# Recommender attention on one core: the user stage keeps the rows of 128 users whole, in three SBUF buffers, and reads their sums in place

## The chip, the cores and the metric

The kernel runs on one core of a Trainium2 chip. The metric is the device time of one execution in microseconds (us), lower is better. A program on one core has engines that run side by side: PE (TensorE, matmuls), DVE (VectorE), ACT (ScalarE), POOL (GpSimd) and SP (SyncE). Each works through its own queue in order, and they wait for each other by semaphores. A transfer by indices ("indirect DMA") is issued by POOL: one instruction fetches one row of a DRAM table for each of 128 partitions.

## What is computed

For 16,384 users there is a history of 100 items and one target item. Each item has a row h of 128 numbers: 64 of an embedding and 2 x 32 that come from an attention over 32 neighbouring items. The core of the reference, cut:

```python
a_sus = _neighbor_attn(E_in, near_full)      # softmax over 32 neighbours, for each item
a_inf = _neighbor_attn(E_out, near_full)
h = concat([E_hist[history], a_sus[history], a_inf[history]])      # 16384 x 100 x 128
t = concat([E_tgt[target], a_inf[target], a_sus[target]])          # 16384 x 128
x = h * t[:, None, :]
z = relu(einsum('bld,hd->blh', x, W1) + b1)
scores = einsum('blh,h->bl', z, W2[0])
exp_A = exp(scores) * ((history != target[:, None]) & (history != 0))
denom = sum(exp_A, -1) ** 0.5
s = sum(h * (exp_A / denom[:, None])[..., None])                   # one number over all users
pred = cosine(broadcast(s), t);  return sigmoid(pred)
```

Since s is a sum over all of a row's 128 numbers too, a history item enters it only by the sum of its row, weighted by its attention.

## The kernel before

**Table stage (lines 111 to 238).** For each item the attention over its neighbours is computed, and a row of W = 129 numbers is written to a DRAM table: the row's sum first, then its 128 numbers. The change does not touch this stage.

**User stage (lines 249 to 399).** Users are taken 128 at a time, one on each partition; there are UC = 128 such batches, called "users" c below. The 100 history items of a batch are taken in NG = 25 groups of LG = 4. A step s is one group: c, g = divmod(s, 25), 3,200 steps in all. The program's order on each engine is written out by hand in the loop at line 377 (a manual schedule: each engine gets its instructions in the order in which the loop names them). For a step:

- `gather(s)` (line 299): four indirect DMAs on POOL, one for each item, bring 128 rows of 129 numbers into an SBUF tile `h` of the pool `u_h`. The pool has HBUF = 20 such tiles, so POOL can be twenty groups ahead, and then waits until the group twenty steps back has been read.
- `turn(s)` (line 316): PE transposes the four blocks of 128 x 128 (without the sum's column) into one PSUM tile `hT_ps`; the pool `ps_t` has three, shared with two small uses.
- `times_target(s)` (line 322): DVE multiplies the tile by the target's transposed row (`xT`, line 325, called a "product" below), and copies the four sums into `hsum` (line 328). That copy is the last reader of the tile `h`.
- `hidden(s - 3)` (line 335, LAG = 3): PE multiplies by W1 (`z_ps`, line 337, issued as two matmuls) and ACT applies the relu (line 339).
- `scored(s - 6)` (line 341): PE multiplies by W2 into one row of the PSUM tile `bank` (line 345, two matmuls).

So a step has eight matmuls on PE with eight weight loads. Once for each user there are the target's row (`target_rows`, a gather on POOL; `target_work`), and, when its 25 groups are scored, `weights`, `exponents` and `ended`: the exponentials of the scores, the mask, their sum, and their product with `hsum` (line 369).

An instruction carries one semaphore wait. Where it has to wait for more, the further waits stand ahead of it in its queue as an instruction of their own, a "separate wait". In the program before, POOL has one ahead of nearly each group's first gather (the tile's readers on DVE, beside PE), PE one for each group's transposes, DVE one for over half of its products, ACT some.

Of the kernel before, what the change touches and what calls it, by code (L numbers as in the profile page):

```python
# [10 lines left out]
F32 = mybir.dt.float32  # L11
# [3 lines left out]
AF = mybir.ActivationFunctionType  # L15
# [3 lines left out]
P = 128  # L19
# [4 lines left out]
D = 128  # L24
# [19 lines left out]
LG = 4  # L44
NG = L // LG
W = 1 + D
LAG = 3
M = 2
HBUF = 20

# [3 lines left out]
def kernel(  # L54
# [56 lines left out]
    with (  # L111
# [137 lines left out]
    with (  # L249
        tc.manual_schedule(engines={E.PE, E.Activation, E.DVE, E.SP, E.Pool}),  # L250
        tc.tile_pool(name="u_in", bufs=4) as u_in,
        tc.tile_pool(name="u_t", bufs=3) as u_t,
        tc.tile_pool(name="u_h", bufs=HBUF) as u_h,
        tc.tile_pool(name="u_x", bufs=6) as u_x,
        tc.tile_pool(name="u_z", bufs=6) as u_z,
        tc.tile_pool(name="u_s", bufs=3) as u_s,
        tc.tile_pool(name="ps_t", bufs=3, space=bass.MemoryType.PSUM) as ps_t,
        tc.tile_pool(name="ps_z", bufs=3, space=bass.MemoryType.PSUM) as ps_z,
        tc.tile_pool(name="ps_s", bufs=2, space=bass.MemoryType.PSUM) as ps_s,
    ):  # L260
        users, hists = {}, {}
        rows, got, hT, xT, z = {}, {}, {}, {}, {}

        def history_of(i):
            hists[i] = u_in.tile([P, BSUB, L], I32, name="hidx")
            nc.sync.dma_start(hists[i], hist_v[i])

        def target_rows(c):
            t = u_t.tile([P, D], F32, name="t")
            nc.gpsimd.indirect_dma_start(  # L270
                out=t,
                out_offset=None,
                in_=ttab[0:ITEMS, :],
                in_offset=bass.IndirectOffsetOnAxis(ap=tidx[:, c : c + 1], axis=0),
            )
            users[c] = {"t": t, "hidx": hists[c // BSUB][:, c % BSUB, :]}

        def target_work(c):
            u = users[c]
            t = u["t"]  # L280
            tT_ps = ps_t.tile([P, LG, P], F32, name="hT_ps")
# [14 lines left out]
            u["keep"] = keep  # L296
            u["hsum"] = u_s.tile([P, L], F32, name="hsum")

        def gather(s):
            c, g = divmod(s, NG)  # L300
            rows[s] = u_h.tile([P, LG, W], F32, name="h")
            got[s] = []
            for q in range(LG):
                l = g * LG + q
                got[s].append(
                    nc.gpsimd.indirect_dma_start(  # L306
                        out=rows[s][:, q, :],
                        out_offset=None,
                        in_=table,
                        in_offset=bass.IndirectOffsetOnAxis(  # L310
                            ap=users[c]["hidx"][:, l : l + 1], axis=0
                        ),
                    )
                )

        def turn(s):
            c, g = divmod(s, NG)
            hT[s] = ps_t.tile([P, LG, P], F32, name="hT_ps")
            for q in range(LG):
                nc.tensor.transpose(hT[s][:, q, :], rows[s][:, q, 1:W], ident)  # L320

        def times_target(s):
            c, g = divmod(s, NG)
            xT[s] = u_x.tile([D, LG, P], F32, name="xT")
            nc.vector.tensor_tensor(  # L325
                xT[s], hT.pop(s), users[c]["tT"].to_broadcast([D, LG, P]), ALU.mult
            )
            copy = nc.vector.tensor_copy(  # L328
                users[c]["hsum"][:, g * LG : (g + 1) * LG],
                rows.pop(s)[:, :, 0:1].rearrange("p q o -> p (q o)"),  # L330
            )
            for one in got.pop(s):
                tc.declare_no_dep(copy.ins, one.ins, reason="TensorE has read the row")

        def hidden(s):
            z_ps = ps_z.tile([HID, LG, P], F32, name="z_ps")
            nc.tensor.matmul(z_ps, w1T, xT.pop(s), start=True, stop=True)  # L337
            z[s] = u_z.tile([HID, LG, P], F32, name="z")
            nc.scalar.activation(z[s], z_ps, AF.Relu, bias=b1_sb)  # L339

        def scored(s):
            c, g = divmod(s, NG)
            if g == 0:
                users[c]["bank"] = ps_s.tile([NG, LG, P], F32, name="bank")
            nc.tensor.matmul(  # L345
                users[c]["bank"], pick[:, g, :], z.pop(s), start=g == 0, stop=g == NG - 1
            )

        def weights(c):
            flat = u_t.tile([NG, LG, P], F32, name="flat")  # L350
            nc.scalar.copy(flat, users[c].pop("bank"))  # L351
            users[c]["flat"] = flat

        def exponents(c):
            flat = users[c].pop("flat")
            score = ps_t.tile([P, LG, P], F32, name="hT_ps")
# [20 lines left out]
        for s in range(last + 2 * LAG + 6):  # L377
# [15 lines left out]
            done, left = divmod(s - 2 * LAG - NG, NG)  # L393
# [93 lines left out]
```

## Time and profile before

| what | value |
|---|---|
| time, median of 3 runs | 36161.68 us (36157.8 to 36170.7) |
| the profiled execution's own time | 36158.99 us |
| its span in the profile | 36157.2 us |
| busy in the span | POOL 25713.0 us (71%), PE 9955.5 (28%), DVE 6910.6 (19%), ACT 2692.6 (7%) |
| mean granted TensorE clock | 0.854 |

How to read the rows that follow. In the page's slices, each digit is an engine's busy share in a fortieth of the span, in tenths. A row of a group is: line, engine, operation, output<-inputs with shapes, xcount | busy us in all, mean ns of one | idle time of the engine just before these instructions, and what ended most of it. A row of the timeline is: start, duration, engine, line, operation, count, and in brackets the idle time before it with what ended it. "issue" means that the engine waited for nothing that the profile shows, "remote" that the releaser is not known. PE's rows are in two parts, PEld for weight loads and PE for matmuls. Ends of matmuls are modelled.

### The profile page before, as it was taken

The page shows a single profiled execution, that of the slowest core. Times are in us where ns is not written, and L with a number is a line of the kernel's source. Part 1 is how long each engine was busy: PE and PEld are TensorE (multiplying, and loading weights), DVE is VectorE, ACT ScalarE, POOL GpSimd, SP SyncE. Part 2 cuts the span into 40 slices and gives each one's busy share as a digit, 9 for nine tenths or more (in the row PEclk, how much of TensorE's full clock was granted, in tenths as well). Part 3 has the DMA queues.
Part 4 walks back from the last instruction along what each step waited for, and adds up shares of the span by engine and source line. Part 5 has one row for each costly group of instructions (what it writes and reads, how often), then busy time and mean ns, then how long its engine had stood idle before and what let it go on. Part 6 is the DMA issues. An engine that isn't in the chain of part 4 may idle for free.

```text
span 36157.2 us, 104181 instructions
## 1 busy us (share of the span) xinstructions
PE 9955.5 (28%) x26243; PEld 3219.9 (9%) x26243; DVE 6910.6 (19%) x9965; ACT 2692.6 (7%) x5700; POOL 25713.0 (71%) x25446
## 2 busy tenths in 40 slices
PE   0000000000000000000255555555555555555555
PEld 0000000000000000000011111111111111111111
DVE  2222222222222222222111111111111111111111
ACT  0000000000000000000011111111111111111111
POOL 7777777777777777777666666666666666666666
PEclk9999999999999999999877777777777777777777
DMA  1111111111111111111111111111111111111111
GB/s 42 29 27 27 27 28 29 27 27 27 28 29 28 27 27 28 27 29 25 40 47 47 47 47 47 47 46 47 47 47 47 46 47 46 47 47 47 46 46 43
DMA packets 1027956, 1362.32 MB, mean 38 GB/s; under 512 B 559904, under 2 KB 614432, under 8 KB 1027360
## 3 DMA queue, kind: packets, MB, share of 16 engines
q0 software_dynamic: 814080, 1265.42, 14.4%
q10 hardware_dynamic: 151056, 51.51, 0.8%
q1 hardware_dynamic: 62224, 38.72, 0.4%
q8 instruction: 218, 3.57, 0.0%
q14 instruction: 378, 3.10, 0.0%
HBM read 1315.31 MB, written 51.50 MB: 38 GB/s over the span
## 4 chain that ended last, share of the span: by engine, by line
POOL 37%; another core or an unknown queue 29%; PE 18%; issue 13%; DVE 2%; ACT 1%; DMA 0%; POOLq 0%; SPq 0%; ACTq 0%; DVEq 0%
POOL v L144 37%; PE z_ps L337 7%; PE bank L345 6%; PE hT_ps L320 5%; DVE xT L325 1%; ACT z L339 1%; DVE hsum L328 0%; DMA v<-in_egeo_dram,nidx 0%; PE hT_ps L358 0%; POOL h L306 0%; PE hT_ps L282 0%; ACT flat L351 0%; DVE tT L284 0%; DVE keep L293 0%
## 5 line engine op out<-in xcount | busy, mean ns | idle before, releaser
L306 POOL DMA_INDIRECT h<-table,hidx x12800 | 12107.2, 946 | 6300.4 <-issue 3830.4
L144 POOL DMA_INDIRECT v<-in_egeo_dram,nidx x12512 | 13484.1, 1078 | 4013.5 <-issue 3964.1
L325 DVE TENSOR_TENSOR xT<-hT_ps,tT 128x512 f32<-128x512 f32 x3200 | 2198.7, 690 | 15477.9 <-remote 9681.0
L282 PE MATMUL hT_ps<-ident,t 128*128 128x128 f32 x128 | 46.3, 362 | 17780.0 <-DMA t<-ttab,tidx 17522.1
L337 PE MATMUL z_ps<-xT,w1T 128*128 128x512 f32 x6400 | 4177.9, 741 | 1833.5 <-ACT z L339 1463.2
L320 PE MATMUL hT_ps<-ident,h 128*128 128x128 f32 x12800 | 2520.1, 328 | 5521.0 <-DVE xT L325 3984.9
L345 PE MATMUL bank<-z,pick 128*25 128x512 f32 x6400 | 3978.8, 709 | 0.0
L339 ACT ACTIVATE z<-z_ps,b_sb 128x512 f32<-128x512 f32 x3200 | 2149.8, 687 | 15996.4 <-remote 7924.9
L159 DVE TENSOR_TENSOR prod<-v,own_ps 128x4096 f32<-128x4096 f32 x196 | 864.4, 4410 | 12916.3 <-DMA v<-in_egeo_dram,nidx 12850.6
L320 PEld LDWEIGHTS hT_ps<-ident,h 128*128 128x128 f32 x12800 | 1621.4, 163 | 8660.4 <-DVE xT L325 4994.7
L282 PEld LDWEIGHTS hT_ps<-ident,t 128*128 128x128 f32 x128 | 19.1, 149 | 17919.3 <-issue 17586.5
L176 ACT ACTIVATE ex<-sc,top 128x32 f32<-128x32 f32 x782 | 227.8, 291 | 16993.6 <-DVE top L170 12332.7
L192 DVE TENSOR_TENSOR wv<-v,ex 128x1024 f32<-128x1024 f32 x782 | 1378.3, 1875 | 315.9 <-ACT ex L176 299.5
L337 PEld LDWEIGHTS z_ps<-xT,w1T 128*128 128x128 f32 x6400 | 1175.1, 230 | 2056.4 <-ACT z L339 1647.9
L166 DVE TENSOR_REDUCE sc<-prod 128x128 f32<-128x4096 f32 x196 | 864.4, 4410 | 6.7
L200 DVE TENSOR_REDUCE att<-wv 128x128 f32<-128x4096 f32 x196 | 864.1, 4409 | 6.0
L345 PEld LDWEIGHTS bank<-z,pick 128*25 128x25 f32 x6400 | 433.4, 109 | 3095.3 <-issue 3095.3
L328 DVE COPY hsum<-h 128x4 f32<-128x4 f32 x3200 | 568.9, 178 | 0.0
L358 PE MATMUL hT_ps<-ident,flat 25*128 25x25 f32 x512 | 65.8, 249 | 1051.5 <-ACT flat L351 714.5
L270 POOL DMA_INDIRECT t<-ttab,tidx x128 | 121.1, 946 | 65.9 <-issue 64.1
L358 PEld LDWEIGHTS hT_ps<-ident,flat 25*128 25x128 f32 x512 | 51.5, 170 | 1190.1 <-ACT flat L351 777.2
L176 ACT ACTIVATION_READ_ACCUMULATOR ex<-sc,top 128x1 f32 x782 | 146.0, 187 | 0.0
(55 smaller groups left out, 855.7 us busy)
## 6 DMA issues: line engine op xcount, KB each, us to landing
h<-table,hidx POOLq DMA_INDIRECT x12800
v<-in_egeo_dram,nidx POOLq DMA_INDIRECT x12512
table<-row ACTq DMA_DIRECT2D x22, 1096.5 KB
own<-in_egeo_dram SPq DMA_DIRECT2D x23, 544.0 KB
row<-in_ehist_dram SPq DMA_DIRECT2D x23, 544.0 KB
ttab<-in_etgt_dram ACTq DMA_DIRECT2D x1, 12500.0 KB
ttab<-row ACTq DMA_DIRECT2D x22, 544.0 KB
hidx<-in_history_dram SPq DMA_DIRECT2D x32, 200.0 KB
```

Of the source, the lines that this page charges most:

```text
L144: nc.gpsimd.indirect_dma_start(out=v[:, m, k].rearrange("p t d -> p (t d)"), out_offset=None, in_=egeo, in_offset=bass.IndirectOffsetOnAxi ...
L159: nc.vector.tensor_tensor(prod[:, 0:n].rearrange("p m k t d -> p m k (t d)"), v.rearrange("p m k t d -> p m k (t d)"), own_ps[:, 0:n].to_b ...
L166: nc.vector.tensor_reduce(sc[:, 0:n].rearrange("p m t k -> p m k t"), prod[:, 0:n], AX.X, ALU.add)
L192: nc.vector.tensor_tensor(wv[:, m, t].rearrange("p d k -> p k d"), subs[b]["v"][:, m, :, t, :], ex[:, m, t, :].rearrange("p (k o) -> p k o ...
L200: nc.vector.tensor_reduce(att[:, 0:n], wv[:, 0:n], AX.X, ALU.add)
L306: nc.gpsimd.indirect_dma_start(out=rows[s][:, q, :], out_offset=None, in_=table, in_offset=bass.IndirectOffsetOnAxis(ap=users[c]["hidx"][: ...
L320: nc.tensor.transpose(hT[s][:, q, :], rows[s][:, q, 1:W], ident)
L325: nc.vector.tensor_tensor(xT[s], hT.pop(s), users[c]["tT"].to_broadcast([D, LG, P]), ALU.mult)
L328: copy = nc.vector.tensor_copy(users[c]["hsum"][:, g * LG : (g + 1) * LG], rows.pop(s)[:, :, 0:1].rearrange("p q o -> p (q o)"),)
L337: nc.tensor.matmul(z_ps, w1T, xT.pop(s), start=True, stop=True)
L339: nc.scalar.activation(z[s], z_ps, AF.Relu, bias=b1_sb)
L345: nc.tensor.matmul(users[c]["bank"], pick[:, g, :], z.pop(s), start=g == 0, stop=g == NG - 1)
```

## The change

- `h` is now a tile of a whole user, 100 rows of 129 numbers on each partition, and there are HOLD = 3 of them. A gather writes its row into it.
- The copy into `hsum` is gone. `ended(c)` reads the sums in place, in the user's tile. That read is now the last reader, so that the waits of the gathers of user c + 3 for the rows of user c come down to one, ahead of its first gather.
- The tiles `hT`, `z_ps`, `xT` and `z` are no longer taken from pools but are fixed rings of TB = 2, ZP = 3, XB = 4 and ZB = 4. The target's transposition and the exponents use a PSUM tile of their own (`e_ps`).
- The order of a step on PE is now `scored(s - 5)`, `hidden(s - 2)`, `turn(s)` instead of `turn(s)`, `hidden(s - 3)`, `scored(s - 6)`. With the rings' sizes, what an instruction has to wait for is then already implied by an earlier wait in its own queue, or is the one wait that it carries; `declare_no_dep` tells the framework which dependences are implied (`in_order`: one engine writes both in its order).

The diff, cut to its core:

```diff
-LAG = 3
 M = 2
-HBUF = 20
+HOLD = 3
+TB = 2
+XB = 4
+ZP = 3
+ZB = 4
+LH = 2
+LS = LH + ZP
...
-        tc.tile_pool(name="u_h", bufs=HBUF) as u_h,
-        tc.tile_pool(name="u_x", bufs=6) as u_x,
-        tc.tile_pool(name="u_z", bufs=6) as u_z,
+        tc.tile_pool(name="u_h", bufs=HOLD) as u_h,
+        tc.tile_pool(name="u_r", bufs=1) as u_r,
...
+        hT = [ps_r.tile([P, LG, P], F32, name=f"hT{i}") for i in range(TB)]
+        z_ps = [ps_r.tile([HID, LG, P], F32, name=f"z_ps{i}") for i in range(ZP)]
+        xT = [u_r.tile([D, LG, P], F32, name=f"xT{i}") for i in range(XB)]
+        z = [u_r.tile([HID, LG, P], F32, name=f"z{i}") for i in range(ZB)]
+        def in_order(one, other):
+            tc.declare_no_dep(one.ins, other.ins, reason="one engine writes both in its order")
...
         def gather(s):
             c, g = divmod(s, NG)
-            rows[s] = u_h.tile([P, LG, W], F32, name="h")
...
+            if g == 0:
+                rows[c] = u_h.tile([P, L, W], F32, name="h")
+            for l in range(g * LG, (g + 1) * LG):
+                one = nc.gpsimd.indirect_dma_start(
+                    out=rows[c][:, l, :],
...
+                got[c, l] = one
+                if c >= HOLD:
+                    tc.declare_no_dep(
+                        one.ins,
+                        turned[c - HOLD, l].ins,
+                        reason="the sums of these users are read after their rows are turned",
+                    )
...
-            hT[s] = ps_t.tile([P, LG, P], F32, name="hT_ps")
-            for q in range(LG):
-                nc.tensor.transpose(hT[s][:, q, :], rows[s][:, q, 1:W], ident)
+                turned[c, l] = nc.tensor.transpose(hT[s % TB][:, q, :], rows[c][:, l, 1:W], ident)
+                if s >= TB:
+                    in_order(turned[c, l], turned[(s - TB) // NG, (s - TB) % NG * LG + q])
...
-            copy = nc.vector.tensor_copy(
-                users[c]["hsum"][:, g * LG : (g + 1) * LG],
-                rows.pop(s)[:, :, 0:1].rearrange("p q o -> p (q o)"),
-            )
...
-            nc.vector.tensor_tensor(ea, ea, u["hsum"], ALU.mult)
+            sums = nc.vector.tensor_tensor(
+                ea, ea, rows.pop(c)[:, :, 0:1].rearrange("p l o -> p (l o)"), ALU.mult
+            )
+            for l in range(L):
+                tc.declare_no_dep(
+                    sums.ins, got.pop((c, l)).ins, reason="TensorE has read the row"
+                )
...
                 gather(s)
+            if 0 <= s - LS < last:
+                scored(s - LS)
+            if 0 <= s - LH < last:
+                hidden(s - LH)
+            if s < last:
                 turn(s)
                 times_target(s)
-            if 0 <= s - LAG < last:
-                hidden(s - LAG)
-            if 0 <= s - 2 * LAG < last:
-                scored(s - 2 * LAG)
```

More of the change, by code (lines that the diff above doesn't have):

```diff
@@ L252 @@
         tc.tile_pool(name="u_t", bufs=3) as u_t,
-        tc.tile_pool(name="u_h", bufs=HBUF) as u_h,
-        tc.tile_pool(name="u_x", bufs=6) as u_x,
-        tc.tile_pool(name="u_z", bufs=6) as u_z,
+        tc.tile_pool(name="u_h", bufs=HOLD) as u_h,
+        tc.tile_pool(name="u_r", bufs=1) as u_r,
         tc.tile_pool(name="u_s", bufs=3) as u_s,
-        tc.tile_pool(name="ps_t", bufs=3, space=bass.MemoryType.PSUM) as ps_t,
-        tc.tile_pool(name="ps_z", bufs=3, space=bass.MemoryType.PSUM) as ps_z,
+        tc.tile_pool(name="ps_r", bufs=1, space=bass.MemoryType.PSUM) as ps_r,
+        tc.tile_pool(name="ps_e", bufs=1, space=bass.MemoryType.PSUM) as ps_e,
         tc.tile_pool(name="ps_s", bufs=2, space=bass.MemoryType.PSUM) as ps_s,
@@ L261 @@
         users, hists = {}, {}
-        rows, got, hT, xT, z = {}, {}, {}, {}, {}
+        rows, got, turned, times, first, second = {}, {}, {}, {}, {}, {}
+        hT = [ps_r.tile([P, LG, P], F32, name=f"hT{i}") for i in range(TB)]
[4 more added lines that the diff above has]
+            tc.declare_no_dep(one.ins, other.ins, reason="one engine writes both in its order")
         def history_of(i):
@@ L280, in target_work @@
             t = u["t"]
-            tT_ps = ps_t.tile([P, LG, P], F32, name="hT_ps")
+            tT_ps = ps_e.tile([P, LG, P], F32, name="e_ps")
             nc.tensor.transpose(tT_ps[:, 0, :], t, ident)
@@ L296, in target_work @@
             u["keep"] = keep
-            u["hsum"] = u_s.tile([P, L], F32, name="hsum")
         def gather(s):
             c, g = divmod(s, NG)
-            rows[s] = u_h.tile([P, LG, W], F32, name="h")
-            got[s] = []
+            if g == 0:
[3 more added lines that the diff above has]
+                    out=rows[c][:, l, :],
+                    out_offset=None,
+                    in_=table,
+                    in_offset=bass.IndirectOffsetOnAxis(
+                        ap=users[c]["hidx"][:, l : l + 1], axis=0
+                    ),
+                )
[6 more added lines that the diff above has]
+                    )
@@ L303, in gather, with turn @@
+        def turn(s):
+            c, g = divmod(s, NG)
             for q in range(LG):
                 l = g * LG + q
[L305 to L312, printed above, removed]
-                    )
-                )
@@ L335, in hidden @@
[L335 to L339, printed above, removed]
+            times[s] = nc.vector.tensor_tensor(
+                xT[s % XB], hT[s % TB], users[c]["tT"].to_broadcast([D, LG, P]), ALU.mult
+            )
+            for q in range(LG - 1):
+                tc.declare_no_dep(
+                    times[s].ins, turned[c, g * LG + q].ins, reason="TensorE turns them in order"
+                )
@@ L341, in scored, with hidden @@
+            if s >= XB:
+                in_order(times[s], times.pop(s - XB))
+        def hidden(s):
+            first[s] = nc.tensor.matmul(
+                z_ps[s % ZP], w1T, xT[s % XB], start=True, stop=True
+            )
+            if s >= ZP:
+                in_order(first[s], first.pop(s - ZP))
+            second[s] = nc.scalar.activation(z[s % ZB], z_ps[s % ZP], AF.Relu, bias=b1_sb)
+            if s >= ZB:
+                in_order(second[s], second.pop(s - ZB))
         def scored(s):
@@ L345, in scored @@
             nc.tensor.matmul(
-                users[c]["bank"], pick[:, g, :], z.pop(s), start=g == 0, stop=g == NG - 1
+                users[c]["bank"], pick[:, g, :], z[s % ZB], start=g == 0, stop=g == NG - 1
             )
@@ L355, in exponents @@
             flat = users[c].pop("flat")
-            score = ps_t.tile([P, LG, P], F32, name="hT_ps")
+            score = ps_e.tile([P, LG, P], F32, name="e_ps")
             for q in range(LG):
@@ L376 @@
         target_work(0)
-        for s in range(last + 2 * LAG + 6):
+        for s in range(last + LS + 6):
             c, g = divmod(s, NG)
@@ L384 @@
                 gather(s)
+            if 0 <= s - LS < last:
[3 more added lines that the diff above has]
+            if s < last:
                 turn(s)
                 times_target(s)
-            if 0 <= s - LAG < last:
-                hidden(s - LAG)
-            if 0 <= s - 2 * LAG < last:
-                scored(s - 2 * LAG)
             if s < last and g == 15 and c + 1 < UC:
                 target_work(c + 1)
-            done, left = divmod(s - 2 * LAG - NG, NG)
+            done, left = divmod(s - LS - NG, NG)
             if 0 <= done < UC and left == 0:
```

10 lines of the change are left out of this document (3 added, 7 removed).

## The prediction

> **What bounds the kernel now.** I read the page first: the shares by slice and the groups.
>
> ```profile
> span 36157.2 us, 104181 instructions
> PE   0000000000000000000255555555555555555555
> POOL 7777777777777777777666666666666666666666
> L306 POOL DMA_INDIRECT h<-table,hidx x12800 | 12107.2, 946 | 6300.4 <-issue 3830.4
> L270 POOL DMA_INDIRECT t<-ttab,tidx x128 | 121.1, 946 | 65.9 <-issue 64.1
> ```
>
> The first half of the span is the stage that builds the table. It is not touched. The user stage, where PE works, issues 12,800 + 128 row gathers on POOL. How fast could POOL issue them? That is in the timeline of POOL alone, here the first and the last history gather of the stage and one run of gathers with the stall behind it.
>
> ```profile
> 17530.95 0.95 POOL L306 DMA_INDIRECT h<-table,hidx  x1 [3.94 <-DMA hidx<-in_history_dram]
> ...
> 25014.49 0.94 POOL L306 DMA_INDIRECT h<-table,hidx  x1 [2.36 <-PE hT_ps L320]
> 25015.74 0.95 POOL L306 DMA_INDIRECT h<-table,hidx  x1 [0.31 <-issue]
> ...
> 25048.27 0.94 POOL L306 DMA_INDIRECT h<-table,hidx  x1 [0.30 <-issue]
> 25054.00 0.94 POOL L306 DMA_INDIRECT h<-table,hidx  x1 [4.79 <-PE hT_ps L320]
> ...
> 36092.54 0.95 POOL L306 DMA_INDIRECT h<-table,hidx  x1 [0.30 <-issue]
> ```
>
> From 25014.49 to 25048.27 there are 27 steps: 1.2511 us a gather. The stage's 12,927 steps would take 16,173 us at that pace; they took 36092.54 - 17530.95 = 18,561.6. So POOL stalls for 2,389 us, 18.7 us for each of 128 users, whose 101 gathers need 126.4 us. These stalls are waits for a buffer of rows: POOL is twenty groups (of four rows) ahead and waits for PE and DVE. A change that gives POOL more buffers helps only if PE and DVE can keep POOL's pace of 5.06 us a group (126.4 / 25). So the next view is what PE and DVE do while POOL runs. The timeline of all engines near the stage's start, where POOL's twenty buffers are still free and POOL waits for nobody:
>
> ```profile
> 17564.00 0.69 DVE L325 TENSOR_TENSOR xT<-hT_ps,tT 128x512 f32<-128x512 f32 x1 [5.45 <-PE hT_ps L320]
> ...
> 17600.27 0.69 DVE L325 TENSOR_TENSOR xT<-hT_ps,tT 128x512 f32<-128x512 f32 x1 [20.85 <-remote]
> ...
> 17601.02 1.12 PE L320 MATMUL hT_ps<-ident,h 128*128 128x128 f32 x4 [12.56 <-issue]
> ...
> 17606.57 0.69 ACT L339 ACTIVATE z<-z_ps,b_sb 128x512 f32<-128x512 f32 x1 [21.71 <-remote]
> ...
> 17607.31 2.08 PE L337 MATMUL z_ps<-xT,w1T 128*128 128x512 f32 x2 [5.17 <-issue]
> ...
> 17609.31 1.90 PE L345 MATMUL bank<-z,pick 128*25 128x512 f32 x2
> ...
> 17622.67 0.69 DVE L325 TENSOR_TENSOR xT<-hT_ps,tT 128x512 f32<-128x512 f32 x1 [21.63 <-remote]
> ...
> 17628.98 0.69 ACT L339 ACTIVATE z<-z_ps,b_sb 128x512 f32<-128x512 f32 x1 [21.73 <-remote]
> ```
>
> Up to 17564.00 DVE has made six products in 33 us, at POOL's pace. Then it falls back. PE's work for a group is over at 17611.2, and DVE's operand has stood in PSUM for long, since PE may be three groups ahead (three PSUM tiles). Yet DVE starts its next product 22.40 us after the last one, and ACT its next 22.41 us after its last, both idle and with a releaser that the profile can't name ("remote"). What is late is the news from PE that its instructions have ended. 22.40 us for the 16 PE instructions of a group (eight weight loads, eight matmuls) is 1.40 us each. Two windows of the groups view (122 us near the start, then 34.8 us of the run shown above) say how much gets through while POOL runs:
>
> ```profile
> L325 DVE TENSOR_TENSOR xT<-hT_ps,tT 128x512 f32<-128x512 f32 x6 | 4.2, 692 | 121.2 <-remote 107.4 <-PE hT_ps L320 13.8
> L306 POOL DMA_INDIRECT h<-table,hidx x94 | 88.9, 946 | 31.5 <-issue 30.0 <-DMA h<-table,hidx 1.2 <-PE bank L345 0.3
> ...
> L325 DVE TENSOR_TENSOR xT<-hT_ps,tT 128x512 f32<-128x512 f32 x6 | 4.1, 692 | 17.4 <-PE z_ps L337 8.3 <-remote 7.6 <-PE hT_ps L320 1.4
> L306 POOL DMA_INDIRECT h<-table,hidx x28 | 26.5, 946 | 10.6 <-issue 7.3 <-PE hT_ps L320 2.4 <-remote 0.6
> ```
>
> Six products in 122 us (20.3 us each) where POOL has run without a break; six in 34.8 us right after a stall. And where POOL has ended for good, in the timeline behind the last gather and in the groups from 36100 to 36140:
>
> ```profile
> 36095.31 0.68 DVE L325 TENSOR_TENSOR xT<-hT_ps,tT 128x512 f32<-128x512 f32 x1
> ...
> 36098.80 1.90 PE L345 MATMUL bank<-z,pick 128*25 128x512 f32 x2
> ...
> 36133.35 0.69 DVE L325 TENSOR_TENSOR xT<-hT_ps,tT 128x512 f32<-128x512 f32 x1 [1.65 <-PE hT_ps L320]
> ...
> 36135.76 0.69 DVE L325 TENSOR_TENSOR xT<-hT_ps,tT 128x512 f32<-128x512 f32 x1 [1.65 <-PE hT_ps L320]
> ...
> 36136.52 1.04 PE L345 MATMUL bank<-z,pick 128*25 128x512 f32 x2
> ...
> L325 DVE TENSOR_TENSOR xT<-hT_ps,tT 128x512 f32<-128x512 f32 x15 | 10.4, 692 | 26.0 <-PE hT_ps L320 26.0
> ```
>
> Here a group takes 2.41 us (36133.35 to 36135.76), fifteen of them lie between 36100 and 36140, with the same instructions and the same waits. So the stage swings between two paces: while POOL gathers, PE's ends reach DVE and ACT at 20 to 22 us a group, after a credit of some groups that a stall has bought; while POOL stands still, a group takes 2.41 us. POOL's short stalls are what lets the rest catch up. They are not waste that more buffers remove.
>
> **The change, part by part.** The time is made against the profiled execution, 36158.99 us (span 36157.2 and 1.8 around it), 2.7 below the median of 36161.68; 0.2% of that is 72 us, about what a measurement can tell.
>
> *Instructions.* The hsum copies go, and in the built programs the separate waits go from 3,198 to none on PE (transposes), 1,796 to none on DVE, 380 to none on ACT (relu) and 3,149 to 94 on POOL.
>
> ```profile
> L325 DVE TENSOR_TENSOR xT<-hT_ps,tT 128x512 f32<-128x512 f32 x3200 | 2198.7, 690 | 15477.9 <-remote 9681.0
> L328 DVE COPY hsum<-h 128x4 f32<-128x4 f32 x3200 | 568.9, 178 | 0.0
> ```
>
> The copies' 569 us lie beside 15,478 us of idle time that DVE has ahead of its products: worth nothing. The same idle time covers the strided read of the sums, once a user; without that cover the 128 reads would still be a few tens of us. The waits that go cost PE and DVE no time where POOL is still (2.41 us a group with them). What they cost while POOL runs no row shows alone. The bounds: nothing, if the 1.40 us belong to PE's 16 instructions, which all stay; everything that POOL loses, 2,389 us, if they belong to the waits. I take nothing, since the sixteen account for the 22.40 and since the tail has the same waits at 2.41; the other end is a rival.
>
> *Buffers.* POOL no longer waits group by group. It writes three users' rows freely, then needs, ahead of each further user c + 3, the sums' read of user c, which DVE does behind the tenth product of user c + 1. So there is one stall a user instead of about four short ones (18.7 / 4.79), and a run is 126.4 us long. Behind POOL's one wait all its gathers are queued, those of the target rows too; nobody lacks rows meanwhile, since two users and more lie ready.
>
> *Products in a run of 126.4 us.* Six in the first 34.8, then (126.4 - 34.8) / 20.3 = 4.5: 10.5. PE's lead is shorter (two transposed groups instead of three, and the first matmul now stands ahead of the next transposes): I take one off, 9.5. Below: 5.6, if each costs 22.40 from the start. Above: 14, if the credit after a long stall is twice that of a short one.
>
> *The stall.* 25 - 9.5 = 15.5 groups at 2.41 are 37.4 us; 3 more for its start (1.8 us from the last gather's end at 36093.49 to the first product at 36095.31, and PE's bank matmuls at first 1.90 us a pair instead of 1.04): 40.5 us a user, against 18.7 before.
>
> *The sum.* Three users filled freely: 3 x 126.4 = 379 us, in which some 23 products get done (six by 17564, then one in 20.3); the read that POOL waits for stands behind the 35th: 12 x 2.41 + 3 = 32. Then 125 users at 126.4 = 15,800, with 124 stalls of 40.5 = 5,022 between them. When POOL ends, 55.5 groups are left (3,200 less the 3,135 ahead of user 124's read, less 9.5): 134 us, and 21 from the last product at 36135.76 to the end of the span. 17,531 + 379 + 32 + 15,800 + 5,022 + 134 + 21 = 38,919; with 1.8 around it **38,921 us**, given as 38,920, 7.6% slower.
>
> *A rule beside this.* The Trainium skill, "Perfetto Trace Analysis", section "Optimization Strategy", says that the same gap repeating on the engine that should be saturated can mean too little memory for the next tile, buffer count among it. By that rule three whole users of rows would end POOL's stalls, and the sum would be the first rival's below. The trace does not agree: with all twenty buffers free the products came 22.40 us apart.
>
> **The rivals.**
>
> *The waits are the cause (faster).* If the separate waits make PE's news late, the pace under a running POOL falls below 5.06 us a group, POOL never stalls, and the stage is bound by its gathers: 36,159 - 2,389 = 33,770, less some 20 us of shorter tail: 33,750. That decides from 5.06 us downward. For it: up to 17564.00 the products kept POOL's pace, and just there DVE's products begin to wait separately, since their first six buffers are used up. Against it: the tail's 2.41. The Trainium skill, "TensorE: Matmul & The Clock Gate", section "The cost: per-tile semaphore tail", has 26.3 ns for each increment that a matmul makes on completion; by that figure the six increments of a group are an estimated 0.16 us, nothing would be late, and this rival's time would follow. The trace disagrees where POOL runs (22.40 us a group).
>
> *No memory in the pace.* If a long stall buys as much for each us as the short ones do now, 18.7 us a user still do: 36,160, no change. Against it: the pace falls from 5.8 us (34.8 / 6) to 20.3 us as a run goes on.
>
> *The stall at the slow clock.* If PE stays at the pace of 17601 (1.12 + 2.08 + 1.90 = 5.10 us a group) through the stall, it is 15.5 x 5.10 + 3 = 82 us, and the time 44,070. Against it: at the tail the bank pair is back at 1.04.
>
> **How the numbers follow.** Forecast 0.81, waits 0.13, no memory 0.03, slow clock 0.03. The forecast's own bounds: 14 products in a run give a stall of 11 x 2.41 = 26.5 and 37,190; 5.6 in a run give 19.4 x 2.41 + 3 = 50, and four of those groups at 5.10 another 11: 61, and 41,460. The range is 37,100 to 41,450; it leaves out the waits' case and the slow clock's. Faster 0.14 (the waits, and a third of "no memory"), same 0.02, slower 0.84.
>
> **What would show it.** In the timeline of POOL: runs of 101 gathers 1.25 us apart, and one idle time of about 40 us ahead of each user's first gather. In the timeline of DVE: products about 20 us apart late in such a run, 2.4 us apart in the idle time. The products' idle time should still be put down to "remote". It is wrong if the products follow at 5 us or less while POOL runs (the waits were the cause), or if the stall is near 19 us.

## The result, and the profile after

The changed kernel takes 39,756.5 us (median of 5, 39,739 to 39,761) against 36,162.8 (median of 5) before: a ratio of 1.0993, 95% interval 1.0981 to 1.1004. It is slower, as forecast; the profiled execution (39,756.5 us) is 835 us above the sum of 38,921. One thing is needed to read the later numbers: the runs came in two conditions that no kernel set, told apart by the table stage, which all kernels share. In the first (the result, E1 to E4, E11) a gather of that stage takes 1.40 us on average and before takes 36,160 to 36,250 us; in the second (E5 to E10, E12) it takes 1.25 us throughout and before takes 31,867 to 31,896. Every run is set against the kernel before in its own condition.

The page of the changed kernel (span, slices, groups), and from the waits view of POOL in the window from 18,000 to 39,000 us its largest row (engine, line, what it waited for: us in all, times, longest):

```profile
span 39754.7 us, 92550 instructions
PE   0000000000000000004444444444444444444444
POOL 7777777777777777775555555555555555555554
L315 POOL DMA_INDIRECT h<-table,hidx x12800 | 12098.5, 945 | 9812.3 <-PE hT L335 5941.7
L149 POOL DMA_INDIRECT v<-in_egeo_dram,nidx x12512 | 13482.0, 1078 | 4013.7 <-issue 3962.9
L341 DVE TENSOR_TENSOR xT<-hT,tT 128x512 f32<-128x512 f32 x3200 | 2208.3, 691 | 19613.8 <-remote 13032.4
```

```profile
POOL h L315 <- PE hT L335: 5744.9, 121, 50.8
```

POOL's slices fall from 6 to 5 in the user stage, PE's from 5 to 4. The gathers' own time is the same (12,098.5 us); the idle time ahead of them grew from 6,300.4 to 9,812.3 us. 5,744.9 / 121 = 47.5 us a stall, once a user. One of them in the timelines of POOL and of DVE, with the products ahead of it:

```profile
24917.42 0.94 POOL L315 DMA_INDIRECT h<-table,hidx  x1 [45.93 <-PE hT L335]
...
25042.25 0.94 POOL L315 DMA_INDIRECT h<-table,hidx  x1 [0.30 <-issue]
25091.10 0.94 POOL L315 DMA_INDIRECT h<-table,hidx  x1 [47.91 <-PE hT L335]
```

```profile
25016.21 0.69 DVE L341 TENSOR_TENSOR xT<-hT,tT 128x512 f32<-128x512 f32 x1 [21.71 <-remote]
25039.31 0.69 DVE L341 TENSOR_TENSOR xT<-hT,tT 128x512 f32<-128x512 f32 x1 [22.41 <-remote]
25056.81 0.69 DVE L341 TENSOR_TENSOR xT<-hT,tT 128x512 f32<-128x512 f32 x1 [16.81 <-remote]
25059.09 0.69 DVE L341 TENSOR_TENSOR xT<-hT,tT 128x512 f32<-128x512 f32 x1 [1.59 <-remote]
25060.52 0.69 DVE L341 TENSOR_TENSOR xT<-hT,tT 128x512 f32<-128x512 f32 x1 [0.74 <-PE hT L335]
25063.85 0.69 DVE L341 TENSOR_TENSOR xT<-hT,tT 128x512 f32<-128x512 f32 x1 [2.64 <-PE hT L335]
25066.31 0.69 DVE L341 TENSOR_TENSOR xT<-hT,tT 128x512 f32<-128x512 f32 x1 [1.77 <-PE hT L335]
```

Late in the run the products are 22 to 23 us apart, as forecast. But when POOL stops at 25043.2, no product starts for 13.6 us: POOL and DVE stand still, and PE too, once it has ended the group that it had begun (about 25044.8). Products follow quickly only from 25059.09 on, and from 25063.85 on they are 2.46 us apart. The windows view, of the products alone, counts them in that run and in its stall (DVE busy us, number; clock; DMA share, GB/s):

```profile
24917.50:25043.20 125.70, 7.61 (x11) 0.63 0.21 53
25043.20:25091.10 47.90, 9.69 (x14) 0.84 0.01 2
```

Eleven products in the run, fourteen in the stall, and in the stall hardly any data move (2 GB/s against 53): PE's news is late although no gather is under way.

### The profile page after: what moved, and what is told of

It reads as the page before. It is cut to its first block, busy times and chain, and to the rows that moved or that the text cites. A ratio compares the mean times of both kernels' runs of the same rounds, so it can differ in the third digit from the quotient of the medians.

```text
span 39754.7 us, 92550 instructions
## 1 busy us (share of the span) xinstructions
PE 9563.9 (24%) x26243; PEld 3505.2 (9%) x26243; DVE 6686.4 (17%) x6765; ACT 2743.4 (7%) x5700; POOL 25702.0 (65%) x25446
## 4 chain that ended last, share of the span: by engine, by line
another core or an unknown queue 37%; PE 16%; DVE 2%; issue 1%; POOL 0%; DMA 0%; ACT 0%; SPq 0%; ACTq 0%
PE z_ps L352 7%; PE bank L365 6%; PE hT L335 3%; DVE xT L341 1%; PE e_ps L378 0%; DVE keep L305 0%; DVE tT L296 0%; DVE keep L304 0%; POOL h L315 0%; DVE tsum L298 0%; DVE idf L303 0%; PE e_ps L294 0%; DMA table<-row 0%; DMA h<-table,hidx 0%
## 5 line engine op out<-in xcount | busy, mean ns | idle before, releaser
L315 POOL DMA_INDIRECT h<-table,hidx x12800 | 12098.5, 945 | 9812.3 <-PE hT L335 5941.7
L149 POOL DMA_INDIRECT v<-in_egeo_dram,nidx x12512 | 13482.0, 1078 | 4013.7 <-issue 3962.9
L352 PE MATMUL z_ps<-xT,w1T 128*128 128x512 f32 x6400 | 4358.4, 768 | 12636.7 <-DVE xT L341 9750.2
L341 DVE TENSOR_TENSOR xT<-hT,tT 128x512 f32<-128x512 f32 x3200 | 2208.3, 691 | 19613.8 <-remote 13032.4
L365 PE MATMUL bank<-z,pick 128*25 128x512 f32 x6400 | 3803.6, 680 | 0.0
L335 PE MATMUL hT<-ident,h 128*128 128x128 f32 x12800 | 2284.0, 309 | 17.8 <-DMA h<-table,hidx 16.6
L335 PEld LDWEIGHTS hT<-ident,h 128*128 128x128 f32 x12800 | 1901.5, 163 | 2197.9 <-issue 2097.8
L162 ACT COPY own_ps<-own 128x64 f32<-128x64 f32 x391 | 82.3, 210 | 57.3 <-issue 49.7
```

The costliest lines, as they stand in the source:

```text
L149: nc.gpsimd.indirect_dma_start(out=v[:, m, k].rearrange("p t d -> p (t d)"), out_offset=None, in_=egeo, in_offset=bass.IndirectOffsetOnAxi ...
L315: one = nc.gpsimd.indirect_dma_start(out=rows[c][:, l, :], out_offset=None, in_=table, in_offset=bass.IndirectOffsetOnAxis(ap=users[c]["hi ...
L335: turned[c, l] = nc.tensor.transpose(hT[s % TB][:, q, :], rows[c][:, l, 1:W], ident)
L341: times[s] = nc.vector.tensor_tensor(xT[s % XB], hT[s % TB], users[c]["tT"].to_broadcast([D, LG, P]), ALU.mult)
L352: first[s] = nc.tensor.matmul(z_ps[s % ZP], w1T, xT[s % XB], start=True, stop=True)
L365: nc.tensor.matmul(users[c]["bank"], pick[:, g, :], z[s % ZB], start=g == 0, stop=g == NG - 1)
```

## The experiments

**E1: the new order, rings and waits, with before's buffers.** The changed kernel with 20 tiles of one group and the copies into `hsum` instead of three whole users:

```diff
-HOLD = 3
+TG = 1
+HBUF = 20
...
-            if g == 0:
-                rows[c] = u_h.tile([P, L, W], F32, name="h")
+            if g % TG == 0:
+                held.append((c, g // TG))
+                rows[c, g // TG] = u_h.tile([P, TG * LG, W], F32, name="h")
...
+                copy = nc.vector.tensor_copy(
+                    users[c]["hsum"][:, a:b],
+                    rows.pop((c, g // TG))[:, 0 : b - a, 0:1].rearrange("p l o -> p (l o)"),
+                )
```

> The changed kernel's rings, order and waits, with the rows of one group in a tile and twenty tiles again, and the copies of the sums (so POOL waits group by group). Pace theory (PE's ends reach DVE and ACT late while POOL gathers; only POOL's stalls let them catch up, and what the change did is to make one long stall a user of many short ones): as before within 1%, 35,800 to 36,500, POOL stalling some 19 us a user in gaps of about 5 us. Waits theory (the separate waits on PE, DVE and ACT make them late): 33,750 to 34,500. If the shorter rings and the new order made the change slow: about 39,700.

Measured: 36,231 us, ratio 1.0014 (1.0004 to 1.0023). The separate waits, the rings and the new order gain nothing (0.14% slower); the waits' rival falls.

**E2: the whole users alone.** Before, with its order, rings and waits, and only the row buffers changed (sums read in place):

```diff
-HBUF = 20
+HOLD = 3
...
-            rows[s] = u_h.tile([P, LG, W], F32, name="h")
+            if g == 0:
+                rows[c] = u_h.tile([P, L, W], F32, name="h")
```

> The kernel before with the rows of 128 users whole in three tiles and the sums read in place, its own rings, order and separate waits on PE, DVE and ACT kept. Pace theory: 39,300 to 40,200, one stall of 43 to 50 us a user. If the rings and the order made the change slow: about 36,160. If the waits theory holds in part: slower than the changed kernel by over 1% (above 40,200).

Measured: 39,507 us, ratio 1.0921 (1.0899 to 1.0943). The waits view of POOL in the same window:

```profile
POOL h L304 <- PE hT_ps L323: 5545.1, 122, 47.7
```

45.5 us a stall, once a user: this part of the change alone makes nearly the whole loss.

**E3: 75 tiles of one group.** Before with as much memory for rows as the change has, given back group by group:

```diff
-HBUF = 20
+HBUF = 75
```

> The kernel before with 75 tiles of one group instead of 20: as much memory as the changed kernel has, released group by group. Pace theory: the depth only moves POOL's lead; 36,000 to 36,500, gaps of about 5 us on POOL from some 400 us into the stage on. Depth theory (far lead, or rows far apart, is what costs): about 39,700. Memory theory (too few buffers cause POOL's stalls): about 33,800.

Measured: 37,747 us, ratio 1.0434 (1.0413 to 1.0455), between the two expectations: a miss. Its waits view (same window, up to 37,000) names another wait:

```profile
POOL t L270 <- PE z_ps L337: 1957.6, 121, 46.1
POOL h L306 <- PE hT_ps L320: 1015.1, 214, 12.1
```

POOL waits once a user for a buffer of the target's row, 16 us a time: it gathers the target row of user c + 1 at group 5 of user c, and its buffer is freed by the target work at group 15 of user c - 3, 65 groups back, so that 75 tiles can't be used. Such a stall again lets many tiles come free at once (the windows view counts nine products in the 18.4 us of one), and a run of about 85 gathers follows. That this wait makes the loss is read from the trace; E7 was to show it and came in the other condition.

**E4: no gathers by index.** The changed kernel with the history's rows brought by SP in plain transfers of 128 consecutive rows (this leaves out the lookup of the history's items):

```diff
-                one = nc.gpsimd.indirect_dma_start(
-                    out=rows[c][:, l, :],
...
+                at = (c * L + l) * P % (ITEMS - P)
+                one = nc.sync.dma_start(rows[c][:, l, :], table[at : at + P, :])
```

> Leaves out the gathers by index of the history: SP brings 128 rows that follow each other in the table by a plain transfer, as many transfers of the same bytes into the same places, the rest as in the changed kernel. Pace theory, POOL's gathers being what delays PE's news: products 2.4 to 2.7 us apart, or at SP's pace if that is slower, and no product that stands 20 us behind its transposes; with PE as the bound the stage is 3,200 x 2.45 = 7,840 us and the time near 25,400. If any transfers of rows, whoever issues them, delay PE's news: products late in a user 20 us apart and idle time put down to remote.

Measured: 25,487 us in one run. From its groups view, and two products of its timeline:

```profile
L335 DVE TENSOR_TENSOR xT<-hT,tT 128x512 f32<-128x512 f32 x3200 | 2213.8, 692 | 5440.2 <-PE hT L329 5440.2
```

```profile
21502.30 0.69 DVE L335 TENSOR_TENSOR xT<-hT,tT 128x512 f32<-128x512 f32 x1 [1.77 <-PE hT L329]
21504.76 0.69 DVE L335 TENSOR_TENSOR xT<-hT,tT 128x512 f32<-128x512 f32 x1 [1.77 <-PE hT L329]
```

The same PE instructions, as many rows of the same size at over twice the rate (the windows view has 109 GB/s from 20,000 to 25,000 us, and 39 for the changed kernel from 20,000 to 39,000), and a group takes 2.46 us throughout with no "remote" at all. So in this condition the news is late beside POOL's gathers by index and not beside these transfers. E4 changes three things at once, though: who issues, whether by index, and whether the rows lie together in the table. Which of them matters it doesn't show.

**A second theory.** Why 14 us of nothing behind a run, where before's stalls of some 5 us had products in them? The table stage has an answer that the prediction overlooked, in POOL's timeline of the changed kernel near its start and at 10 ms, and around the end of the user stage's first fill:

```profile
12.74 0.94 POOL L149 DMA_INDIRECT v<-in_egeo_dram,nidx  x1 [0.30 <-issue]
13.99 0.95 POOL L149 DMA_INDIRECT v<-in_egeo_dram,nidx  x1 [0.30 <-issue]
...
10001.91 1.10 POOL L149 DMA_INDIRECT v<-in_egeo_dram,nidx  x1 [0.30 <-issue]
10003.31 1.10 POOL L149 DMA_INDIRECT v<-in_egeo_dram,nidx  x1 [0.30 <-issue]
...
17529.00 0.94 POOL L315 DMA_INDIRECT h<-table,hidx  x1 [4.15 <-DMA hidx<-in_history_dram]
...
17923.39 1.09 POOL L315 DMA_INDIRECT h<-table,hidx  x1 [0.30 <-issue]
17924.78 1.10 POOL L315 DMA_INDIRECT h<-table,hidx  x1 [0.30 <-issue]
17982.17 0.94 POOL L315 DMA_INDIRECT h<-table,hidx  x1 [56.28 <-PE hT L335]
```

A fresh run of gathers goes at 1.25 us each, and after some 180 of them in the user stage (208 in before's table stage) POOL itself is held to 1.40 us (0.15 longer in each instruction); over the table stage the mean is (13,482.0 + 4,013.7) / 12,512 = 1.398. Theory two: something behind POOL serves a gather in 1.40 us, POOL issues one each 1.25, and the 0.15 us are a debt that grows until a bound (180 x 0.15 = 27 us, 208 x 0.15 = 31) holds POOL back. PE's news passes the same place and is late as long as debt stands. Three counts from the first condition fit. The burst of products that ends the late news, counted to the first product that follows another within 4 us, comes about 5 us behind before's runs of some 28 gathers (28 x 0.15 = 4.2), about 16 us behind runs of 101 (15.2), and 27.5 us behind the first fill of 303 (the bound, 27). Over all runs after which POOL stood still long enough to see it, the medians are 5.4 us for 21 to 30 gathers in before and 15.9 us for 101 in the changed kernel. Theory one is the prediction's: news is late because POOL runs, 1.40 us for each PE instruction.

**E5 to E8** were to tell them apart and came in the second condition, where theory two's debt doesn't arise.

E5, a memset of a tile that nobody reads behind each history gather of the changed kernel:

```diff
+    pause = const.tile([P, 128], F32, name="pause")
...
+                nc.gpsimd.memset(pause, 0.0)
```

> The changed kernel with one more POOL instruction behind each history gather: a memset of a 128x128 tile that nobody reads (0.20 us busy in the trace of the changed kernel, so an estimated 1.455 us a gather instead of 1.251; 147 us a user instead of 126.4). Theory one (PE's ends are late because POOL is running): the runs get 20.6 us longer, one more product fits into each, the stall stays near 44 us: 39,757 + 125 x (20.6 - 2.4) = 42,030. Theory two (each gather leaves 1.40 us of work on the way that PE's news takes, POOL issues one each 1.251 us, and the 0.15 us a gather pile up: 5 us after 28 gathers, 16 us after 101): at 1.455 us a gather nothing piles up, PE's news is on time, POOL hardly stalls, and although each gather costs more the time is 17,531 + 12,927 x 1.455 + some 150 = 36,490 (36,200 to 36,900).

Measured: 32,976 us, ratio 1.0348 (1.0327 to 1.0369), hardly a stall: here the memset only makes each gather longer (1.34 us).

E6, five buffers of 13 groups instead of three users, the sums copied:

> The changed kernel with five buffers of 13 groups (52 rows of each of 128 users) instead of three of whole users, and the sums copied once a buffer: POOL stalls twice a user, behind runs of some 50 gathers (63 us). Theory two (debt of 0.15 us a gather): the news comes 7.5 to 8 us after such a run's end, 8.2 of 12.5 products lie in the run, the stall is 8 + 4.3 x 2.41 = 18.4 us, 37 us a user instead of 46.8: 39,757 - 125 x 10 = 38,500. Theory one with a fixed 15 us until the news comes: a stall of 25.4 us, 51 a user: 40,280. Depth alone (65 groups of buffers, nearly as many as the 75 of the changed kernel): 39,400 or more.

Measured: 31,905 us, ratio 1.0012 (1.0001 to 1.0022).

E7, `HBUF = 60` in before:

> The kernel before with 60 buffers of one group instead of 20. With 75 it took 37,747, and the waits of POOL there stood 1,990 us at the gather of the target rows (on a buffer of target rows that is freed 65 groups behind POOL), 46 to 15 us each, after which several groups came free at once. If that wait made the loss, 60 buffers never reach it and the time is that of before, 36,100 to 36,250. If depth itself costs: 36,163 + 40/55 x 1,584 = 37,315.

Measured: 31,908 us, ratio 1.0013 (1.0002 to 1.0023).

E8, E1's kernel with `xT`, `z`, `w1T` and `pick` in bfloat16:

> The order, rings and waits of the changed kernel with 20 buffers of one group (36,231 us as run before), with products, hidden units, the first layer's weights and the picking matrix in bfloat16: 12 instead of 16 PE instructions a group (the arithmetic is less exact). If each PE instruction costs 1.40 us while POOL gathers, the late pace falls from 22.4 to 16.8 us a group, 7.5 instead of 5.6 products of a user come at that pace, and the stall falls from 18.7 to about 12.6 us a user: 35,380. If POOL's gathers owe 1.40 us each whatever PE does, the user stage can't get below 128 x 141.4 us and the time lies between 35,675 and 36,230. No gain at all (36,230) if the number of PE's instructions doesn't matter.

Measured: 31,824 us, ratio 0.9986 (0.9977 to 0.9996).

None of the four has a stall of POOL over 3 us, so the run lengths and PE instructions that they vary could not matter; on those questions they are void. What they do show is what the next run was made for.

**E9: the changed kernel itself in the second condition.**

> The changed kernel itself once more, against the kernel before. In the second series of runs the table stage's gathers took 1.249 us each throughout, where the first series and the runs of the result had 1.25 at the start and then 1.40 on average; PE's ends were on time there, POOL never stalled in the user stage, and before took 31,867 us. Theory two (the lateness of PE's news is the debt of gathers that are issued faster than they are served): where this run's table stage has 1.249 us a gather, the changed kernel has no stall either and takes 31,820 to 31,910, no change; where it has 1.40, it takes 39,760 again. Theory one (PE's ends are late because POOL is running): 39,760 less the shorter table stage, 37,900, in either case.

Measured: 31,904 us, ratio 1.0011 (1.0002 to 1.0021). Its page, POOL's waits from 16,000 to 31,700, and its DVE timeline:

```profile
L315 POOL DMA_INDIRECT h<-table,hidx x12800 | 12077.8, 944 | 3901.7 <-issue 3867.5
L149 POOL DMA_INDIRECT v<-in_egeo_dram,nidx x12512 | 11805.3, 944 | 3826.5 <-issue 3752.7
L341 DVE TENSOR_TENSOR xT<-hT,tT 128x512 f32<-128x512 f32 x3200 | 2211.7, 691 | 13549.8 <-PE hT L335 13549.8
```

```profile
POOL h L315 <- PE hT L335: 4.3, 14, 0.3
```

```profile
25003.73 0.69 DVE L341 TENSOR_TENSOR xT<-hT,tT 128x512 f32<-128x512 f32 x1 [4.29 <-PE hT L335]
25008.72 0.69 DVE L341 TENSOR_TENSOR xT<-hT,tT 128x512 f32<-128x512 f32 x1 [4.29 <-PE hT L335]
```

The table stage's gathers take (11,805.3 + 3,826.5) / 12,512 = 1.249 us, none is held back, and in the user stage POOL gathers at the same 1.25 us as ever while PE's news is on time: a product each 5.0 us, no "remote", no stall. So a running POOL does not by itself delay PE; theory one falls as it was put. Before's time in this condition (31,868 us) leaves no room for stalls either, though no trace of it was kept: there is nothing that the buffers could save or lose, and the changed kernel is 0.1% slower.

The traces of the two conditions differ in one thing more. The last table of a page gives the time in us from a gather's issue to its landing, which is made from records of semaphore updates. Here is its row in the changed kernel's page of the first condition, and then in E9's:

```profile
h<-table,hidx POOLq DMA_INDIRECT x12800
h<-table,hidx POOLq DMA_INDIRECT x12800, 2.5
```

In the first condition the time is missing, because most of the records are: counted in the packed traces, 48,943 updates by transfers against 409,429 in E9 (16 a transfer). They are complete in the first 50 us of the table stage, and from 100 us on there are fewer than two a gather. So "remote" can also mean a lost record, and what shows that news is late is the start times of the products. A rival is left that no run here tests: that the records themselves are what is slow in the first condition, since every time in this document is that of an execution recorded with its span and clock.

**E10 and E11: the pause at 1.41 us a gather, in both conditions** (E5 with a tile of 128 x 208).

> The changed kernel with a memset of a 128x208 tile behind each history gather (128x128 gave 1.337 us a gather in the second series instead of 1.249; an estimated 1.41 here). Where the table stage's gathers take 1.40 us (first series): theory two, nothing piles up, POOL stalls little, 17,531 + 12,927 x 1.41 + 50 = 35,810, faster than before and 3,900 us faster than the changed kernel without the memset (should the step come out at 1.37, a debt of 0.03 a gather stays and some 800 us with it); theory one, runs 16 us longer and the same stall, 41,400. Where they take 1.249 (second series): both have no stall, 15,665 + 12,927 x 1.41 + 20 = 33,910.

> The changed kernel with a memset of a 128x208 tile behind each history gather once more, for the condition of the first series (the table stage's gathers at 1.40 us). There, with 1.41 us a gather: theory two, no debt and hardly a stall, 17,531 + 12,927 x 1.417 + 30 = 35,880, 3,870 us less than the changed kernel without the memset; theory one, the same stalls behind longer runs, 41,400. In the condition of the second series (1.249 us) it takes 33,850 as before and tells nothing new.

E10 came in the second condition: 33,850 us (ratio 1.0614, 1.0583 to 1.0645), no stall, as both theories had it. E11 came in the first, one run: 37,282 us, beside 36,245 for before. From its page, POOL's waits from 18,000 to 36,500, and the timelines of POOL and of DVE at the end of a run:

```profile
L149 POOL DMA_INDIRECT v<-in_egeo_dram,nidx x12512 | 13426.2, 1073 | 4071.7 <-issue 4009.3
```

```profile
POOL h L316 <- PE hT L337: 1370.0, 59, 34.2
```

```profile
24977.44 0.95 POOL L316 DMA_INDIRECT h<-table,hidx  x1 [0.16 <-issue]
25012.85 0.95 POOL L316 DMA_INDIRECT h<-table,hidx  x1 [34.17 <-PE hT L337]
```

```profile
24958.41 0.69 DVE L343 TENSOR_TENSOR xT<-hT,tT 128x512 f32<-128x512 f32 x1 [12.07 <-remote]
24970.39 0.69 DVE L343 TENSOR_TENSOR xT<-hT,tT 128x512 f32<-128x512 f32 x1 [11.29 <-remote]
24980.98 1.29 DVE L343 TENSOR_TENSOR xT<-hT,tT 128x512 f32<-128x512 f32 x2 [9.90 <-remote]
24984.69 0.69 DVE L343 TENSOR_TENSOR xT<-hT,tT 128x512 f32<-128x512 f32 x1 [2.42 <-PE hT L337]
```

Each gather costs POOL 0.16 us more, 2,000 us over the stage, and yet the kernel is 2,470 us faster than without the pause. The stalls fall from 121 of 47.5 us to 59 of 23.2 us, the first product behind a run comes 1 to 3 us after its end (24,980.98 against 24,978.4 here) instead of about 13, and late products are 10 to 12 us apart instead of 22. Theory one had 41,400 and falls a second time. Theory two had the direction and the short wait behind a run, but its 35,880 was 1,400 us too low: at a pace just above the service time the news is better, not prompt, and theory two as put has no reason for the products that are still 10 to 12 us apart. Where between 1.41 us and the pace of no wait at all the news becomes prompt is open.

**E12: E8 once more.**

> The version with 20 buffers of one group and 12 instead of 16 PE instructions a group once more, for the condition of the first series (the table stage's gathers at 1.40 us; with 16 instructions it took 36,231 there). If each PE instruction costs 1.40 us while news is late: a late pace of 16.8 us a group, stalls of 12.6 us a user, 35,380. If the gathers' own 1.40 us set the floor: not below 128 x 141.4 us for the user stage, 35,680 or more. If the number of PE's instructions doesn't matter: 36,230. In the condition of the second series (1.249 us) it takes 31,824 as before and tells nothing new.

It came in the second: 31,835 us, ratio 0.9985 (0.9975 to 0.9994), which repeats E8. This is the one version below both kernels. Against the changed kernel (31,904 us in E9) the difference is the tail: behind POOL's last gather it has one product left, the changed kernel 34, at 2.4 us each, since there an instruction of the kernel's end (line 449) stands ahead of them in DVE's queue and waits 168 us for the last gather. Where its 0.15% against the kernel before comes from is open, as no trace of that one was kept in this condition. What it does in the first condition was not seen, nor was it shown whether the number of PE's instructions matters there.

## Why the prediction was right, and where it was not

**The direction and the path of the loss: right.** One stall a user behind a run of 101 gathers, products some 22 us apart late in a run and 2.46 in the stall, the idle time under "remote": all as forecast. E2 shows that the buffers do it, E1 that the waits don't, both in the first condition. The trace that the prediction read was of that condition, and it is luck that the result came in it too: in the second the same change makes 0.1% (E9). Why the news is late, the prediction had wrong: it is not enough that POOL runs.

**The first fill: 18 us short, and 24 at its stall.** 303 gathers took 397 us, not 379, since POOL is held to 1.40 us after 180 of them; the stall behind them was 56.3 us, not 32.

**Products in a run: under-sized.** 11 instead of 9.5, 3 us less of stall.

**The start of the stall: mis-sized, the largest error.** 3 us were taken from the end of before's stage, behind a short run. Behind 101 gathers it is about 13 us. 10 more, less the 3, make 47.5 us out of 40.5. Before's trace had such a case, overlooked: its own first fill, a run of 126 gathers and soon another stall, three times as long as its usual ones (timeline of POOL):

```profile
17695.14 0.95 POOL L306 DMA_INDIRECT h<-table,hidx  x1 [0.30 <-issue]
17710.98 0.94 POOL L306 DMA_INDIRECT h<-table,hidx  x1 [14.90 <-issue]
```


From the first fill's end to the last gather the trace has 814 us more than the sum (6.5 a user), the fill 18, the tail 5, the start 2 less: the 835.

**The 1.40 us: not a fixed price of PE's instructions.** The prediction divided 22.40 us by sixteen PE instructions. The same number stood in the table stage of the page it read: 1.40 us is what a gather takes there once POOL has run for a while. E9 runs the same sixteen instructions beside the same gathers with none of it, so PE's instructions alone don't set it. Why a late group takes just sixteen times 1.40 us stays open: one gather served ahead of each PE instruction's news would give it, but no run varied the number of PE's instructions in the first condition. The sum came out because a run's late pace was measured, not derived.

**"POOL's short stalls are not waste": right, and by theory two in numbers.** 101 gathers at 1.40 us are 141 us of the 145 that a user took before (126.4 + 18.7): by that theory before's stalls lie where the debt would have had to be paid anyway. After the change a user takes 173 us: for two thirds of each stall (all but some 16 of 47.5 us) the news is on time again, and POOL waits for groups that PE works off at 2.46 us.

**The rivals.** The waits' case (33,750) fell with E1. "No memory in the pace" is nearer the truth for the stalls that are short against the debt, as before's are, but one wait for a whole user can't be. The slow clock in the stall didn't come: the windows above have 0.84 over it. The rule of the Trainium skill that the prediction weighed ("Perfetto Trace Analysis", section "Optimization Strategy": a repeated gap on the engine to be saturated can mean too few buffers) is not borne out here: more buffers cost 4 to 10% in the first condition and changed 0.1% in the second.

**Not foreseen:** that the whole effect hangs on a condition of the run that the kernel doesn't set, and whose mark is the 1.40 us.

## What to carry to other kernels

When an engine's short stalls are what lets the others catch up, fewer and longer stalls are not the same as less stalling: give buffers back in small pieces, and look at how much work the single wait leaves to be done behind it. Before pricing a delay per instruction, look for the same number in another stage of the same trace; here it stood in the table stage, under another engine. A steady pace that differs between a run's first and its thousandth instruction (1.25 and 1.40 us) hints at a bound behind the engine; then a sum with that pace belongs beside the one with the first. And measure both kernels again at another time: the same change cost 10% in one condition and 0.1% in the other.

## What the runs showed of the hardware

In the first condition, where a long run of indirect gathers starts at 1.25 us each and is then held to 1.40, the news of PE's ended instructions came up to 22 us a group late, and stayed late for 5 to 27 us after POOL had stopped, with hardly any transfer under way. Plain transfers at over twice the rate in the same condition didn't do this (E4), nor did the same gathers in the second condition, where they are not held back (E9). That gathers issued faster than they are served are the cause fits the lengths of the late news and the one run of E11, but it is not shown. An extra POOL instruction behind each gather made the kernel 2,470 us faster in the first condition (E11, one run, against the changed kernel) and 1,950 us slower in the second (E10 against E9).

Whether gathers are held to 1.40 us differed between runs of identical programs (39,757 and 31,904 us for the changed kernel), and the record has both under the same chip number (14: E1 to E4 and E5 to E8). What sets it, what place PE's news and the gathers share, and whether the recording of the traces has a part in it, no run here shows.
